# One reset of the running score sum per attention unit, row maxima turned through DRAM, and a staggered last block in a decoder layer

## The chip, the core and the metric

The kernel runs on one NeuronCore of one Trainium2 chip, as one program in one launch. The metric is the device time of that program in microseconds. The core has five engines that run side by side and wait for each other by semaphores: TensorE (PE, matmuls; PEld is its weight load), VectorE (DVE), ScalarE (ACT), GpSimd (POOL) and SyncE (SP, which here issues all DMAs).

## The reference, cut to what matters

The input x has 2 batches of 2048 tokens with 512 features, all in float32. The layer has three residual steps:

```
x = x + attention(layernorm(x)) @ Wo.T     # 16 heads of 32, rotary angles on Q and K
x = x + gelu(layernorm(x) @ ctx.T) @ ctx   # ctx: 77 rows of 512 for each batch
x = x + clip(layernorm(x) @ sign(W).T * scale + bias, -100, 100)
```

Attention is full (2048 by 2048 scores for each head), with a softmax over the keys.

## The kernel before

For each batch the kernel first projects and then attends; what follows attention is cut into small pieces that run in the background of later work.

*Projection* (`project_batch`). The 16 chunks of 128 tokens are taken in turn: layer norm, transposition, K, Q and V matmuls, `rotate` with the `cos` and `sin` tables (lines 207 to 219), and transposition of Q and K into `att.q` and `att.k`, which hold features on partitions, in four blocks of 512 tokens. The last part (lines 254 to 274) has its TensorE and VectorE order written out by hand.

*Attention* (`Attention.run`). A unit is a block of queries, a group `g` of four heads (their 32 features lie on the four strips of 32 partitions) and a half block of 256 queries: 4 x 4 x 2 = 32 units per batch, 64 in all. A unit takes 8 steps (`STEPS`), and a step works on two chunks of 128 keys, which `chunk(i, c)` gives as key block `i % 4`, first half of the block for steps 0 to 3 and second half for steps 4 to 7. A step has two half steps, one for heads 0 and 1, one for heads 2 and 3. In each half, TensorE computes scores into `st`, ScalarE exponentiates them into `pw` (line 705), GpSimd adds the two key chunks into `sm` (line 707), and TensorE multiplies `pw` by the values (`weigh`, line 583) and sums `sm` with ones (`total`, line 597), both for earlier steps.

The scores are kept as a running sum in PSUM. `lower` (line 545) starts a tile of `st` with minus the row maximum, from a tile `mrow` of three bfloat16 parts on partitions. In the first step that follows, `scores` adds the product with the keys of block 0, and in later steps the product with a *difference* of key blocks (`dk`, made in `key_steps`), so that the same PSUM tile turns into the scores of the next keys. `lower` runs in steps 0 and 4.

The row maxima come from a second product, with queries on partitions (`maxima`, line 459): four matmuls of 512 columns per step into `ps` and four VectorE reductions (line 484) into `mx`. They run `AHEAD` = 10 steps ahead of the scores; the first ten of a batch are done in the projection, in the order in which `open_block` puts them into `due` and `lead` takes them out. When a unit's maxima are complete (the end of step 5), `split_maxima` takes the maximum over the key blocks on VectorE and splits it into three bfloat16 parts on GpSimd (lines 493 to 497), and `turn_maxima` brings them onto partitions: by a transposing DMA from SyncE (line 504), and for the first unit of a batch, on TensorE (line 508).

`divide` takes reciprocals and products at a unit's end (lines 607 to 624). In `run` the orders of TensorE, VectorE, ScalarE and GpSimd are written out by hand, as the statements are emitted. Outside, and for SyncE throughout, a planner orders the instructions, by the order of emission and its own estimate of when each is ready.

*After attention* (`after_attention`, line 312). A generator with a `yield` after each piece: output projection and residual (`add_to_x`), layer norm, the 77 context rows with a GELU from products and a tanh (lines 387 to 405), and the sign-weight product with scale, bias, clip and residual (lines 370 to 378). `background` takes pieces from `queue` in the gaps of attention and projection. `side()` gives the engine of the simple operations: GpSimd in general, VectorE in the last `AHEAD` steps of a batch (`free`) and after all attention (`alone`). The four chunks of the last query block of batch 1 go to `tail` instead, one generator each; after attention the last loop of the function runs one piece of each in turn.

*Buffers.* `big` (for `pw`) and `sums` (for `sm`) have three buffers, `ps_t` (for `st`) four and `ps_s` (for `ps`) three.

Of the kernel before, what the change touches and what calls it, by code (L numbers as in the profile page):

```python
# [9 lines left out]
F32 = mybir.dt.float32  # L10
# [6 lines left out]
P = 128  # L17
# [8 lines left out]
HQ = 256  # L26
NU = NB * ND * 2
STEPS = NCH // 2
AHEAD = STEPS + 2
SCALE = 1.0 / math.sqrt(DK)  # L30
EPS = 1e-5
MAX_VAL = 100.0
# [4 lines left out]
def decoder_layer(  # L37
# [48 lines left out]

    x_next = [load_x(0, 0), load_x(0, 1)]
    qkv = load_qkv()
    cos = const.tile([P, NCH, DK // 2], F32, tag="cos", name="cos")
    sin = const.tile([P, NCH, DK // 2], F32, tag="sin", name="sin")  # L90
    nc.sync.dma_start(cos, rope_cos.rearrange("(p c) d -> p c d", p=P))
    nc.sync.dma_start(sin, rope_sin.rearrange("(p c) d -> p c d", p=P))

    ident = const.tile([P, P], F32, tag="ident", name="ident")
    make_identity(nc, ident)
# [7 lines left out]
    nc.scalar.activation(minus_half, ones[:, :CPB], AF.Identity, scale=-0.5)  # L103


    mts = []
    for n in range(2):
        mt = const.tile([P, 2, 4, DK], BF16, tag=f"mt{n}", name=f"mt{n}")
        nc.vector.memset(mt, 0.0)
        mts.append(mt)  # L110

    late = {}

# [63 lines left out]

    def project_batch(b, ahead, att, xnt, wk, wq, wv):  # L180
# [25 lines left out]

        def rotate(ch, a, ps, r):
            half = [P, H, DK // 2]
            cs = cos[:, ch, None, :, None].to_broadcast(half + [2])
            sn = sin[:, ch, None, :].to_broadcast(half)  # L210
# [70 lines left out]

    def side():
        return nc.vector if alone or free else nc.gpsimd


    attending = []
# [25 lines left out]
    def after_attention(b, blk, ot, first, end):  # L312
# [41 lines left out]
        def feed_forward(c, pt):  # L354
            parts = [work_tile([P, D], name, F32R) for name in ("high", "low")]
            parts = [part.rearrange("p (i t) -> p i t", t=P) for part in parts]
            nc.scalar.copy(parts[0], pt)
            nc.vector.tensor_sub(parts[1], pt, parts[0])
            yield True
            pf = bank([P, D], "pf")  # L360
            for k, part in enumerate(parts):
                for i in range(ND):
                    nc.tensor.matmul(  # L363
                        pf,
                        part[:, i, :],
                        wf[:, i, :],
                        start=(k == 0 and i == 0),
                        stop=(k == 1 and i == ND - 1),
                    )
            y = work_tile([P, D], "y")  # L370
            nc.vector.tensor_mul(y, pf, fs)
            yield False
            side().tensor_add(y, y, fb)
            yield False
            side().tensor_scalar(y, y, -MAX_VAL, MAX_VAL, ALU.max, ALU.min)
            side().tensor_add(xs[c], xs[c], y)
            nc.sync.dma_start(tokens(out[b], blk * CPB + first + c), xs[c])
            yield False

# [11 lines left out]
        nc.scalar.copy(h, ph)  # L391
        yield False
        u = work_tile([C, n * P], "u")
        side().tensor_mul(u, h, h)
        yield False
        side().tensor_scalar(u, u, 0.044715, 1.0, ALU.mult, ALU.add)
        side().tensor_mul(u, u, h)
# [4 lines left out]
        side().tensor_scalar(u, u, 1.0, 0.5, ALU.add, ALU.mult)  # L402
        side().tensor_mul(u, u, h)
        yield False
        yield True

# [38 lines left out]
    class Attention:  # L445
# [13 lines left out]
        def maxima(self, n, heads):  # L459
# [25 lines left out]

            return reduce

        def split_maxima(self, u):
            mx = self.mx.pop(u)
            neg = small.tile([P, 2, 4], F32, tag="neg", name="neg")  # L490
            nc.vector.tensor_reduce(neg, mx, AX.X, ALU.max, negate=True)
            mt = mts[u % 2]
            nc.gpsimd.tensor_copy(mt[:, :, :, 0], neg)
            nc.gpsimd.tensor_tensor(neg, neg, mt[:, :, :, 0], ALU.subtract)
            nc.gpsimd.tensor_copy(mt[:, :, :, 1], neg)
            nc.gpsimd.tensor_tensor(neg, neg, mt[:, :, :, 1], ALU.subtract)
            nc.gpsimd.tensor_copy(mt[:, :, :, 2], neg)


        def turn_maxima(self, u):  # L500
            mt = mts[u % 2]
            mrow = small.tile([P, 2, P], BF16, tag="mrow", name="mrow")
            if u > 0:
                nc.sync.dma_start_transpose(mrow, mt.rearrange("p c h d -> p (c h d)"))
            else:
                pt = ps_s.tile([P, 2, P], BF16, tag="s", name="ptm")
                for c in range(2):
                    nc.tensor.transpose(
                        pt[:, c, :], mt[:, c].rearrange("p h d -> p (h d)"), ident_b
                    )  # L510
                nc.vector.tensor_copy(mrow, pt)
            self.mrow[u] = mrow.rearrange("p c q -> p (c q)")

        def key_steps(self):
            self.dk = [None] + [
                const.tile([P, ND, BLK], F32, tag=f"w{n}", name=f"dk{n}") for n in "kqv"
            ]

            def differences(g):
# [12 lines left out]
            for _ in differences(0):  # L534
                pass
            queue.append(others())


        @staticmethod
# [19 lines left out]
        def scores(self, u, i, heads, c):  # L559
            qb, g, hf = self.units[u]  # L560
            kb, kc = divmod(self.chunk(i, c), CPB)
            keys = self.dk[kb] if kb else self.k[kb]
            for h in heads:
                r = self.rows[h]
                nc.tensor.matmul(  # L565
                    self.st[h][:, c, :],
                    keys[r, g, kc * P : (kc + 1) * P],
                    self.q[qb][r, g, hf * HQ : (hf + 1) * HQ],
                    start=False,
                    stop=True,  # L570
                    skip_group_check=True,
                )
# [74 lines left out]
        def run(self):  # L647
# [37 lines left out]
            for t in range(NU * STEPS):  # L685
# [10 lines left out]
                pw = big.tile([P, 4, 2, HQ], F32, tag="s", name="pw")  # L696
                sm = sums.tile([P, 4, HQ], F32, tag="sm", name="sm")
                for heads, others in (((0, 1), (2, 3)), ((2, 3), (0, 1))):
                    if i % NB == 0:
                        self.lower(u, heads)  # L700
                    self.scores(u, i, heads, 0)
                    reduce = self.maxima(t + AHEAD, others)
                    self.scores(u, i, heads, 1)
# [6 lines left out]
                    if heads[0] == 0:  # L710
                        first_half()
                        finish()
                        if u >= NU - ND:
                            background(1)
                        elif t % 2 == 1:
                            background(1, light=True)
                    else:
                        finish()
                        second_half()
                        if prev is not None and prev[1] == STEPS - 1:  # L720
                            finish()
# [15 lines left out]
    xnt = turn(norm(x_next, 0, 0, nc.vector))  # L737
    for b in range(B):
        att = Attention(b)
        project_batch(b, x_next, att, xnt, *qkv)  # L740
        if b == 0:
            late_loads()
        load_ctx(b)
        xnt = att.run()
        if b + 1 < B:
            x_next = att.x_next
            qkv = load_qkv()
    alone.append(True)
# [51 lines left out]
```

## Time and profile before

| | |
|---|---|
| time, median of 3 runs | 2693.01 us (2692.51 to 2693.29) |
| the profiled execution's own time | 2693.15 us |
| its span, first to last instruction | 2691.0 us |
| TensorE busy | 2668.3 us |
| GpSimd, VectorE, ScalarE busy | 1732.8, 1710.0, 1321.0 us |
| projection of batch 0 ends, first L550 | 212.4 us |
| first L550 of batch 1 | 1544.9 us |
| tail, first `po` to the end of the span | 2643.7 to 2691.0 us |
| mean granted TensorE clock | 0.998 |

The profile is of one execution. Times in it are in microseconds from the start of its span. A timeline row gives start, duration, engine, source line, operation, output<-inputs, shapes and count (merged neighbours), and in square brackets the idle time of that engine before it with the instruction that ended the idle time. "L550" is line 550 of the kernel before. A float32 matmul appears as two instructions.

### The profile page before, as it was taken

To read this page: it belongs to the slowest core of one execution; us is meant where nothing else is said; L and a number is where in the kernel's file an instruction comes from. 1 tells how busy PE (TensorE), PEld (TensorE's weight loads), DVE (VectorE), ACT (ScalarE), POOL (GpSimd) and SP (SyncE) were. 2 spreads that over 40 slices of the span, in tenths; PEclk is the share of its full clock that TensorE was granted. 3 is DMA by queue.
4 is the path that set the end of the run, shared out by engine and by line. 5 is a ranking of instruction groups with operands and counts; after the bars stand their busy time and mean duration, and the time that the engine had idled before them with its cause. 6 is when DMAs were issued, how large, how long until landed. Compare 5 with 4: busy or idle time off the path is not lost.

```text
span 2691.0 us, 70222 instructions
## 1 busy us (share of the span) xinstructions
PE 2668.3 (99%) x30756; PEld 1490.3 (55%) x30756; DVE 1710.0 (64%) x2863; ACT 1321.0 (49%) x2394; POOL 1732.8 (64%) x1876
## 2 busy tenths in 40 slices
PE   8999999999999999999999999999999999999998
PEld 4445555555555555555554455555565555555555
DVE  3447777676766766676344477766767667766754
ACT  2115555455546554555422155555555455546553
POOL 3227777567857785677543287766687567857772
PEclk9999999999999999999999999999999999999999
DMA  3010000000000000000201000000000000000000
GB/s 126 24 32 2 5 4 4 4 4 18 20 3 4 12 28 3 4 12 26 73 25 40 5 4 4 4 4 4 4 27 12 4 4 19 19 4 4 19 19 17
DMA packets 38019, 43.54 MB, mean 16 GB/s; under 512 B 20662, under 2 KB 20918, under 8 KB 37712
## 3 DMA queue, kind: packets, MB, share of 16 engines
q1 hardware_dynamic: 37712, 39.05, 4.8%
q8 instruction: 241, 3.95, 0.6%
q14 instruction: 66, 0.54, 0.1%
HBM read 26.58 MB, written 8.39 MB: 13 GB/s over the span
## 4 chain that ended last, share of the span: by engine, by line
PE 98%; DVE 1%; DMA 0%; issue 0%; ACT 0%; POOL 0%; SPq 0%; POOLq 0%; ACTq 0%
PE st L565 23%; PE acc L583 22%; PE ps L472 18%; PE acc L597 8%; PE po L382 4%; PE pk L183 4%; PE pq L183 4%; PE pv L183 4%; PE st L550 3%; PE pf L363 2%; PE pt L345 1%; PE po L408 1%; PE ptqk L191 1%; PE ph L389 1%; PE pt L173 1%; DMA wk<-in_wk_t_dram 0%
## 5 line engine op out<-in xcount | busy, mean ns | idle before, releaser
L707 POOL TENSOR_TENSOR sm<-pw 128x512 f32<-128x512 f32 x1024 | 1295.2, 1272 | 599.5 <-ACT pw L705 596.8
L484 DVE TENSOR_REDUCE mx<-ps 128x1 f32<-128x512 f32 x2048 | 1308.9, 682 | 513.0 <-PE ps L472 509.1
L705 ACT ACTIVATE pw<-st 128x512 f32<-128x512 f32 x2048 | 1111.4, 595 | 947.0 <-PE ps L472 619.4
L472 PE MATMUL ps<-k,q 32*128 32x512 f32 x4096 | 1187.8, 640 | 0.0
L583 PE MATMUL acc<-pw,v 128*32 128x256 f32 x8192 | 655.1, 391 | 0.0
L597 PE MATMUL acc<-sm,ones 128*32 128x128 f32 x7680 | 388.8, 280 | 0.0
L583 PEld LDWEIGHTS acc<-pw,v 128*32 128x32 f32 x8192 | 162.5, 108 | 396.6 <-issue 378.3
L472 PEld LDWEIGHTS ps<-k,q 32*128 32x128 f32 x4096 | 352.4, 183 | 20.2 <-issue 13.8
L597 PEld LDWEIGHTS acc<-sm,ones 128*32 128x32 f32 x7680 | 248.6, 110 | 153.2
L565 PE MATMUL st<-q,dkk 32*128 32x256 f32 x2048 | 291.2, 400 | 0.0
L565 PE MATMUL st<-q,dkq 32*128 32x256 f32 x2048 | 290.0, 400 | 0.0
L565 PE MATMUL st<-q,dkv 32*128 32x256 f32 x2048 | 290.0, 400 | 0.0
L565 PE MATMUL st<-q,k 32*128 32x256 f32 x2048 | 262.8, 375 | 0.0
L565 PEld LDWEIGHTS st<-q,dkk 32*128 32x128 f32 x2048 | 175.8, 184 | 89.5 <-issue 51.3
L565 PEld LDWEIGHTS st<-q,dkq 32*128 32x128 f32 x2048 | 173.0, 184 | 79.9 <-issue 54.1
L565 PEld LDWEIGHTS st<-q,dkv 32*128 32x128 f32 x2048 | 175.0, 184 | 58.6 <-issue 26.3
L565 PEld LDWEIGHTS st<-q,k 32*128 32x128 f32 x2048 | 195.4, 187 | 14.0
L219 POOL TENSOR_TENSOR r<-r 128x512 f32<-128x512 f32 x64 | 81.1, 1268 | 161.8 <-DVE r L218 151.5
L617 DVE RECIPROCAL num<-num 128x128 f32<-128x128 f32 x128 | 120.4, 942 | 53.5 <-ACT num L611 53.5
L137 DVE BATCH_NORM_STATS2 st<-x 128x6 f32<-128x512 f32 x96 | 65.4, 686 | 91.7 <-DMA x<-in_x_dram 91.4
L183 PE MATMUL pk<-wk,xnt 128*128 128x512 f32 x256 | 118.2, 606 | 2.4 <-ACT xnt L175 1.3
L382 PE MATMUL po<-wo,q 128*128 128x512 f32 x256 | 117.4, 603 | 0.0
(109 smaller groups left out, 1784.9 us busy)
## 6 DMA issues: line engine op xcount, KB each, us to landing
x<-in_x_dram SPq DMA_DIRECT2D x64, 256.0 KB, 2.8
out_dram<-x SPq DMA_DIRECT2D x32, 256.0 KB, 2.0
wk<-in_wk_t_dram SPq DMA_DIRECT2D x2, 1024.0 KB, 7.8
wq<-in_wq_t_dram SPq DMA_DIRECT2D x2, 1024.0 KB, 9.9
wv<-in_wv_t_dram SPq DMA_DIRECT2D x2, 1024.0 KB, 5.5
wo<-in_wo_t_dram SPq DMA_DIRECT2D x1, 1024.0 KB, 9.9
wf<-in_wf_t_dram SPq DMA_DIRECT2D x1, 1024.0 KB, 5.0
mrow<-mt SPq DMA_TRANSPOSE x62, 2.3
```

What stands on the lines that cost most here:

```text
L183: nc.tensor.matmul(dst, xnt[:, i, :], w[:, i, :], start=(i == 0), stop=(i == ND - 1))
L219: nc.gpsimd.tensor_add(r[:, 0, a], r[:, 0, a], r[:, 1, a])
L382: nc.tensor.matmul(ps, ot[:, i, cols], wo[:, i, :], start=(i == 0), stop=(i == ND - 1))
L472: nc.tensor.matmul(ps, self.q[qb][self.rows[h], g, q0 : q0 + P], self.k[kb][self.rows[h], g, :], start=True, stop=True,)
L484: nc.vector.tensor_reduce(mx[:, qc, h, kb : kb + 1], ps, AX.X, ALU.max)
L550: nc.tensor.matmul(self.st[h], ones_b[r, :], mrow[r, None, :].to_broadcast([DK, 2, HQ]), start=True, stop=False, skip_group_check=True,)
L565: nc.tensor.matmul(self.st[h][:, c, :], keys[r, g, kc * P : (kc + 1) * P], self.q[qb][r, g, hf * HQ : (hf + 1) * HQ], start=False, stop=Tr ...
L583: nc.tensor.matmul(acc[self.rows[h], 0, :], self.v[self.chunk(i, c)][:, d0 : d0 + DK], pw[:, h, c, :], start=(i == 0 and c == 0), stop=(i ...
L597: nc.tensor.matmul(acc[self.rows[h], 1, part], ones, sm[:, h, part], start=False, stop=(i == STEPS - 1), skip_group_check=True,)
L617: nc.vector.reciprocal(num[:, 1, part], num[:, 1, part])
L705: nc.scalar.activation(pw[:, h], self.st[h], AF.Exp, scale=SCALE)
L707: nc.gpsimd.tensor_add(sm[:, hs, :], pw[:, hs, 0, :], pw[:, hs, 1, :])
```

## The change

It has four parts.

1. `lower` runs in step 0 alone. In step 4 the sum goes on with a wrap difference, the second half of key block 0 minus the first half of key block 3, made on GpSimd once for each head group as its units come up (`wrap_around`).
2. `AHEAD` grows from 10 to 11. `split_maxima` does its first two operations after `neg`, and `turn_maxima` the rest, on VectorE; the turn is called a half step later, in the first half of step 5. It transposes 32 by 32 blocks on VectorE, writes them to DRAM and reads them back with eight DMAs, each of three rows for one head and one half of the queries. The first unit of a batch still goes over TensorE. `mrow` is now a pair of constant tiles.
3. The tables `cos` and `sin` become one tile in the pool `sums`, loaded once for each batch, after the weights.
4. In the tail, a new chunk starts every four turns of the last loop (`STAGGER`). The products of the GELU, and the bias and residual of all but the last chunk, run on GpSimd there (`aside`, `closing`).

```diff
-AHEAD = STEPS + 2
+STAGGER = 4
+AHEAD = STEPS + 3
...
+    def load_angles():
+        angles = sums.tile([P, 2, NCH, DK // 2], F32, tag="sm", name="angles")
+        for n, table in enumerate((rope_cos, rope_sin)):
+            nc.sync.dma_start(angles[:, n], table.rearrange("(p c) d -> p c d", p=P))
+        return angles
...
+    first_mt = zeros([P, 2, 4, DK], "first_mt")
+    mts = [zeros([P, 4, DK // 4], f"mt{n}") for n in range(2)]
+    mrows = [zeros([P, 2, P], f"mrow{n}") for n in range(2)]
+    dram = ctx.enter_context(tc.tile_pool(name="dram", bufs=2, space=bass.MemoryType.DRAM))
...
+    def aside():
+        return nc.vector if free else nc.gpsimd
...
+            closing = side() if first + c == CPB - 1 else aside()
             nc.vector.tensor_mul(y, pf, fs)
             yield False
-            side().tensor_add(y, y, fb)
+            closing.tensor_add(y, y, fb)
             yield False
             side().tensor_scalar(y, y, -MAX_VAL, MAX_VAL, ALU.max, ALU.min)
-            side().tensor_add(xs[c], xs[c], y)
+            closing.tensor_add(xs[c], xs[c], y)
...
-        side().tensor_mul(u, h, h)
+        aside().tensor_mul(u, h, h)
...
         def split_maxima(self, u):
             mx = self.mx.pop(u)
             neg = small.tile([P, 2, 4], F32, tag="neg", name="neg")
             nc.vector.tensor_reduce(neg, mx, AX.X, ALU.max, negate=True)
-            mt = mts[u % 2]
-            nc.gpsimd.tensor_copy(mt[:, :, :, 0], neg)
-            nc.gpsimd.tensor_tensor(neg, neg, mt[:, :, :, 0], ALU.subtract)
-            nc.gpsimd.tensor_copy(mt[:, :, :, 1], neg)
-            nc.gpsimd.tensor_tensor(neg, neg, mt[:, :, :, 1], ALU.subtract)
-            nc.gpsimd.tensor_copy(mt[:, :, :, 2], neg)
+            if u == 0:
+                parts = [first_mt[:, :, :, n] for n in range(3)]
+            else:
+                by_head = mts[u % 2][:, :, 0:6].rearrange("p h (c n) -> p c h n", n=3)
+                parts = [by_head[:, :, :, n] for n in range(3)]
+            nc.vector.tensor_copy(parts[0], neg)
+            nc.vector.tensor_tensor(neg, neg, parts[0], ALU.subtract)
+            self.rest = neg, parts
 
         def turn_maxima(self, u):
+            neg, parts = self.rest
+            nc.vector.tensor_copy(parts[1], neg)
+            nc.vector.tensor_tensor(parts[2], neg, parts[1], ALU.subtract)
+            mrow = mrows[u % 2]
...
-                nc.sync.dma_start_transpose(mrow, mt.rearrange("p c h d -> p (c h d)"))
+                square = small.tile([P, DK], BF16, tag="square", name="square")
+                nc.vector.transpose(square, mts[u % 2].rearrange("p h n -> p (h n)"))
+                rows = dram.tile([P, DK], BF16, tag="rows", name="rows")
+                nc.sync.dma_start(rows, square)
+                by_row = rows.rearrange("(a h n) i -> n a h i", a=4, h=4)
+                for h in range(4):
+                    for c in range(2):
+                        nc.sync.dma_start(
+                            mrow[h * DK : h * DK + 3, c].rearrange("n (a i) -> n a i", a=4),
+                            by_row[3 * c : 3 * c + 3, :, h, :],
+                        )
...
+        def wrap_around(self, g):
+            if self.wrap is None or self.wrap[0] != g:
+                d = small.tile([P, BLK // 2], F32, tag="wrap", name="wrap")
+                nc.gpsimd.tensor_sub(
+                    d, self.k[0][:, g, BLK // 2 :], self.k[NB - 1][:, g, : BLK // 2]
+                )
+                self.wrap = g, d
...
-            keys = self.dk[kb] if kb else self.k[kb]
+            if i == NB:
+                keys = self.wrap[1][:, None, :].to_broadcast([P, ND, BLK // 2])
+                kc = c
+            else:
+                keys = self.dk[kb] if kb else self.k[kb]
...
-                    if i % NB == 0:
+                    if i == 0:
                         self.lower(u, heads)
+                        self.wrap_around(self.units[u][1])
...
+                        if (t + AHEAD) % STEPS == 0 and u + 1 < NU:
+                            self.turn_maxima(u + 1)
...
                         if (t + AHEAD) % STEPS == STEPS - 1 and u + 1 < NU:
                             self.split_maxima(u + 1)
-                            self.turn_maxima(u + 1)
...
-    queue += tail
-    while queue:
+
+    turns = 0
+    while queue or tail:
+        if tail and turns % STAGGER == 0:
+            queue.append(tail.pop(0))
+        turns += 1
         for piece in list(queue):
```

More of the change, by code (lines that the diff above doesn't have):

```diff
@@ L88, in decoder_layer @@
     qkv = load_qkv()
[L89 to L92, printed above, removed]
+    def load_angles():
[3 more added lines that the diff above has]
+        return angles
+    angles = load_angles()
     ident = const.tile([P, P], F32, tag="ident", name="ident")
@@ L103, in decoder_layer, with zeros @@
     nc.scalar.activation(minus_half, ones[:, :CPB], AF.Identity, scale=-0.5)
[L106 to L110, printed above, removed]
+    def zeros(shape, name):
+        t = const.tile(shape, BF16, tag=name, name=name)
+        nc.vector.memset(t, 0.0)
+        return t
+    first_mt = zeros([P, 2, 4, DK], "first_mt")
+    mts = [zeros([P, 4, DK // 4], f"mt{n}") for n in range(2)]
+    mrows = [zeros([P, 2, P], f"mrow{n}") for n in range(2)]
+    dram = ctx.enter_context(tc.tile_pool(name="dram", bufs=2, space=bass.MemoryType.DRAM))
     late = {}
@@ L176, in turn, with project_batch @@
         return xnt
-    def project_batch(b, ahead, att, xnt, wk, wq, wv):
+    def project_batch(b, ahead, att, xnt, angles, wk, wq, wv):
         def times(dst, xnt, w, part=range(ND)):
@@ L208, in rotate @@
             half = [P, H, DK // 2]
-            cs = cos[:, ch, None, :, None].to_broadcast(half + [2])
-            sn = sin[:, ch, None, :].to_broadcast(half)
+            cs = angles[:, 0, ch, None, :, None].to_broadcast(half + [2])
+            sn = angles[:, 1, ch, None, :].to_broadcast(half)
             pairs = ps.rearrange("p (h i t) -> p h i t", i=DK // 2, t=2)
@@ L393, in after_attention @@
         u = work_tile([C, n * P], "u")
-        side().tensor_mul(u, h, h)
+        aside().tensor_mul(u, h, h)
         yield False
-        side().tensor_scalar(u, u, 0.044715, 1.0, ALU.mult, ALU.add)
-        side().tensor_mul(u, u, h)
+        aside().tensor_scalar(u, u, 0.044715, 1.0, ALU.mult, ALU.add)
+        aside().tensor_mul(u, u, h)
         yield False
@@ L401, in after_attention @@
         yield False
-        side().tensor_scalar(u, u, 1.0, 0.5, ALU.add, ALU.mult)
-        side().tensor_mul(u, u, h)
+        aside().tensor_scalar(u, u, 1.0, 0.5, ALU.add, ALU.mult)
+        aside().tensor_mul(u, u, h)
         yield False
@@ L491, in split_maxima @@
             nc.vector.tensor_reduce(neg, mx, AX.X, ALU.max, negate=True)
-            mt = mts[u % 2]
-            nc.gpsimd.tensor_copy(mt[:, :, :, 0], neg)
-            nc.gpsimd.tensor_tensor(neg, neg, mt[:, :, :, 0], ALU.subtract)
-            nc.gpsimd.tensor_copy(mt[:, :, :, 1], neg)
-            nc.gpsimd.tensor_tensor(neg, neg, mt[:, :, :, 1], ALU.subtract)
-            nc.gpsimd.tensor_copy(mt[:, :, :, 2], neg)
-        def turn_maxima(self, u):
[L501 to L505, printed above, removed]
+            if u == 0:
[6 more added lines that the diff above has]
+            self.rest = neg, parts
+        def turn_maxima(self, u):
+            neg, parts = self.rest
+            nc.vector.tensor_copy(parts[1], neg)
+            nc.vector.tensor_tensor(parts[2], neg, parts[1], ALU.subtract)
+            mrow = mrows[u % 2]
+            if u == 0:
                 pt = ps_s.tile([P, 2, P], BF16, tag="s", name="ptm")
@@ L508, in turn_maxima @@
                     nc.tensor.transpose(
-                        pt[:, c, :], mt[:, c].rearrange("p h d -> p (h d)"), ident_b
+                        pt[:, c, :], first_mt[:, c].rearrange("p h d -> p (h d)"), ident_b
                     )
                 nc.vector.tensor_copy(mrow, pt)
+            else:
[10 more added lines that the diff above has]
+                        )
             self.mrow[u] = mrow.rearrange("p c q -> p (c q)")
@@ L519, in key_steps @@
             ]
+            self.wrap = None
             def differences(g):
@@ L561, in scores @@
             kb, kc = divmod(self.chunk(i, c), CPB)
-            keys = self.dk[kb] if kb else self.k[kb]
+            if i == NB:
+                keys = self.wrap[1][:, None, :].to_broadcast([P, ND, BLK // 2])
+                kc = c
+            else:
+                keys = self.dk[kb] if kb else self.k[kb]
             for h in heads:
@@ L739, in decoder_layer @@
         att = Attention(b)
-        project_batch(b, x_next, att, xnt, *qkv)
+        project_batch(b, x_next, att, xnt, angles, *qkv)
         if b == 0:
@@ L747, in decoder_layer @@
             qkv = load_qkv()
+            angles = load_angles()
     alone.append(True)
-    queue += tail
-    while queue:
+    turns = 0
[3 more added lines that the diff above has]
+        turns += 1
         for piece in list(queue):
```

## The prediction

> **What bounds the kernel now.** I read the page first (busy shares, then the chain that ended last), then the timeline of TensorE and VectorE inside one attention unit, then the timeline of the last 47 us, last the SyncE rows.
>
> ```profile
> PE 2668.3 (99%) x30756; PEld 1490.3 (55%) x30756; DVE 1710.0 (64%) x2863; ACT 1321.0 (49%) x2394; POOL 1732.8 (64%) x1876
> ...
> PE 98%; DVE 1%; DMA 0%; issue 0%; ACT 0%; POOL 0%; SPq 0%; POOLq 0%; ACTq 0%
> ```
>
> TensorE is the bound nearly everywhere; 2691.0 - 2668.3 = 22.7 us of its idle time is all that any other engine can give back directly. POOL at 64% is on no chain. The TensorE timeline:
>
> ```profile
> 804.33 0.39 PE L550 MATMUL st<-mrow,ones_b 32*128 32x512 bf16 x2
> ...
> 806.30 0.39 PE L550 MATMUL st<-mrow,ones_b 32*128 32x512 bf16 x2
> ...
> 808.27 0.48 PE L565 MATMUL st<-q,dkk 32*128 32x256 f32 x2
> ...
> 810.12 0.49 PE L565 MATMUL st<-q,dkk 32*128 32x256 f32 x2
> ```
>
> A half step that begins with L550 lasts 806.30 - 804.33 = 1.97 us, twice; the first half without it 810.12 - 808.27 = 1.85, and over the trace second halves without it last 1.90. VectorE in another unit:
>
> ```profile
> 264.67 1.29 DVE L484 TENSOR_REDUCE mx<-ps 128x1 f32<-128x512 f32 x2 [0.57 <-PE ps L472]
> 266.07 0.19 DVE L491 TENSOR_REDUCE neg<-mx 128x8 f32<-128x32 f32 x1
> 266.57 1.29 DVE L484 TENSOR_REDUCE mx<-ps 128x1 f32<-128x512 f32 x2 [0.31 <-PE ps L472]
> ...
> 279.66 0.94 DVE L617 RECIPROCAL num<-num 128x128 f32<-128x128 f32 x1
> 280.52 1.22 DVE L484 TENSOR_REDUCE mx<-ps 128x1 f32<-128x512 f32 x2
> ```
>
> VectorE is idle 0.57 us in a half step, 0.31 in the one that holds `neg`. More than that makes the reductions late, and with three buffers behind `ps` TensorE soon waits: after the two reciprocals of a unit a half of 1.86 lasts 2.22. So VectorE has no slack beyond that gap. The tail:
>
> ```profile
> 2643.66 14.00 PE L382 MATMUL po<-wo,q 128*128 128x512 f32 x32
> ...
> 2667.22 1.10 PE L408 MATMUL po<-ctx,sparev 77*128 77x512 f32 x2 [0.49 <-DVE sparev L403]
> 2672.42 1.12 PE L345 MATMUL pt<-ident,sparek 128*128 128x128 f32 x4 [4.10 <-ACT sparek L339]
> ```
> ```profile
> 2672.00:2676.00 4.00, 3.42 (x15) 3.03 (x16) 1.15 (x7) 3.54 (x7) 0.96 (x2) 0.50 0.01 2
> ```
>
> The four chunks go in step, so TensorE waits for all of them at once (4.10 us); the second view, of four microseconds by engine, shows a granted clock of 0.50 just after (its third number from the end). The last residual ends at 2688.03. The queue that the rows will use:
>
> ```profile
> L504 SPq DMA_TRANSPOSE mrow<-mt x62: 1168/1173/1892, 237.4 to 2606.9; - x62
> ...
> DMA to landing us min/median/max: 2.3/2.3/4.2
> ```
>
> **The change, part by part.** The sum is against the profiled execution: span 2691.0, its own time 2693.15, 2.15 us around it; the median of the three runs, 2693.01, is 0.14 lower.
>
> *Unit-long differences.* Of the two pairs of half steps with L550 in each of 64 units one pair loses it: (1.97 + 1.97) - (1.86 + 1.90) = 0.18 us, x64 = -11.5. The wrap difference is 20 subtractions per batch on POOL, 40 in all; between L707's 1.27 us for 512 columns and L620's 0.46 for 128, about 0.73 each, needed four steps (15 us) later. POOL has 0.6 us free per half step and also loses five small operations per unit (0.20 to 0.22 us each): 0 on the path. Without that cover the cost would be 40 x 0.73 = 29.
>
> *One step more ahead.* AHEAD 11 puts maxima step 10 into the projection, before steps 3 and 7, for 8 more `ps` instructions (1.07 us) and 4 reductions (2.47 us). Today the order there is step 3 (reduced 1536.15 to 1538.6), step 7, the last `pv` at 1539.93, L550 at 1544.88. With a third group ahead of that `pv`, step 7's matmuls wait for step 3's reductions at 1542.5; `pv` starts there, 2.6 us later, in the first batch 3.0, since the sign conversions share VectorE. In attention the removed step gives nothing back: a half lasts 1.85 without maxima and 1.86 with. +5.5.
>
> *Split and turn on VectorE.* After `neg` follow two small operations in the gap of step 4 and two and a transpose in that of step 5. L146 and L148 on VectorE take 0.15 and 0.16, 0.03 apart. First gap: 0.31 left, 0.37 wanted. For a 128x32 transpose no row is near; the zeroing of 128x32 took 0.09, the skill's page "VectorE: DVE Perf Modes", section "The three transpose paths", gives 311 ns for 128x128 bf16, and I take 0.2, since the copy of 128x256 took 0.29. Second gap: 0.57 left, 0.6 wanted. 0.05 us per unit, x64 = +3; the ends are 0 and 0.35 (what 0.3 us too much cost after the reciprocals), +22. Background's `bn_stats` (0.87 with its aggregate) meets these as it met `neg`. For unit 0 the VectorE chain is 0.8 us shorter than POOL's 1.6, behind the late `pv`: 0.
>
> *Rows through DRAM.* SyncE gets nine issues instead of one; plain loads there occupy it 0.33 us each, the transpose 1.17. Backward from L550: `neg` came 6.9 us before it (234.90 to 241.8), the turn comes half a step earlier, at 8.8, the square is done at about 8.2. Write: 2.0 to land (as `out` does); four reads for the first two heads: 3 x 0.33 more, and 2.3; with hops 5.5. Slack 2.7 us; the other four reads land 1.3 later and are needed 2.0 later. Queued behind them on SyncE are x loads and out stores, none due within 3 us. Cost 0; if uncovered, 62 us per us of lateness. Here a rule speaks against the change. The row: landing 2.3, at worst 4.2. The Trainium skill, "DMA: Bandwidth & Descriptors", section "Rules for kernel authors", wants the hardware transpose and calls a rearranged plain DMA 19 times slower: 19 x 2.3 = 44 us, 36 over the slack, x62 = +2200. Each run here stays 64 bytes contiguous, since VectorE transposes the blocks first, so I take the row; no run shows the strided case.
>
> *Angles.* They now share `sums` and are loaded again for batch 1, behind the third weight (issued at 1325.81, 5.5 us to land). The first rotation was at 1332.72; it may be 1 to 2 us late, and `pk` keeps its buffer, of which the fourth successor comes at 1343. SyncE issues two more (0.7 us) ahead of an x load. With the extra semaphores before L550: +0.5, ends 0 and 5.
>
> *The tail.* Emitted four pieces apart, the chunks' `po` stay first in line except where pieces of earlier chunks are ready: two transposes (0.5 each) and two `ph` (1.0 each) enter, so the last `po` ends at 2657.66 + 3.0 = 2660.7. From there one chunk's chain by today's rows: to its normalised x 3.7 (2657.69 to 2661.43), transpose and copy 1.3, `ph` and copy 1.5, products on POOL 0.40 + 2 x 0.46 + 2 x 0.29 (from the 77x512 and 77x256 rows, 1.27 and 0.73) with tanh and hops 2.7, `po` 1.1, statistics and x 3.6, transpose 0.8, parts 1.4, `pf` 2.3, last four on VectorE 2.5: 20.9, so 2681.6, and 1.4 for POOL's 1.27 us bias and residual of earlier chunks in its way: 2683.0 against 2688.03. The row with clock 0.50 bears on this: the skill's page "TensorE: Matmul & The Clock Gate", section "Part 1: The HAM clock gate", halves the clock after an idle window of about 3.4 us. By the rule alone, with no gap that long, the sixteen transposes return from 3.7 us to 2.0 and the tail gains 1.7; by my walk, which counts them at full speed, 5.0. I take -5.5, ends -9 and +1 (POOL's clumsier operations in series).
>
> Sum: -11.5 + 5.5 + 3 + 0.5 - 5.5 = -8.0. 2693.15 - 8.0 = 2685.15; with the 0.14, 2685.0.
>
> **The rivals.** (1) *The removed L550 is eaten*: the extra step 5.5, VectorE 5, angles 1, no gain in the tail: -11.5 + 11.5 = 0, 2693. For it: three small costs, all on engines without slack. Against: the 4.10 us gap. (2) *VectorE becomes the bound of steps 4 to 6*, on the slower side: at 0.35 us per unit the sum is -8 + 19 = +11, 2704. It decides from 0.17 us per unit (-8 + 8). For: the reciprocals' stalls. Against: the gaps nearly fit. (3) *The rows land late*: both landings at 4.2 give 9.4 us for 8.2, +1.2 x 62 = 74, 2759. For: such landings occurred; against: seldom, beside large loads. (4) *The change doesn't do what it says*: if the halves freed of L550 fall only to VectorE's 1.90, 0.14 x 64 = 9, 2687.5.
>
> **How the numbers follow.** The forecast 0.55 (own range 2680 to 2691), rival 4 0.10, rival 1 0.20, rival 2 0.11, rival 3 0.04. About 0.2%, 5.4 us, is what a measurement of this kernel can tell from no change: faster is below 2687.6, slower above 2698.4. Faster: most of the forecast and half of rival 4, 0.57; same 0.27; slower 0.16. The range 2676 to 2697 takes in -9 in the tail and VectorE up to 0.2 us per unit, and leaves out rival 3 and the worst of rival 2.
>
> **What would show it.** L550's bf16 matmuls x256; halves of step 4 at 1.86 and 1.90; the unit of 31.09 us (237.43 to 268.52) near 30.95. L550 from `mrow` of batch 1 at about 1547.5 after that batch's earlier start. No wait of L550 on `mrow`'s DMAs above 0.5 us. The tail from the last attention matmul to the last residual 39 us, not 44, with no clock of 0.50. Wrong: waits of `ps` on `mx` after steps 4 and 5, or L550 waiting for landings in most units.

## The result: 70 us slower

The changed kernel takes 2762.91 us (median of four runs, 2762.36 to 2763.99), the kernel before 2692.8, measured beside it: ratio 1.0261, interval 1.0243 to 1.0278. The prediction was 2685, with a range up to 2697.

The span is 2759.9 us. The busy shares of the page after, and its chain of work that ended last:

```profile
PE 2724.5 (99%) x30500; PEld 1469.8 (53%) x30500; DVE 1835.8 (67%) x3158; ACT 1322.3 (48%) x2394; POOL 1717.2 (62%) x1622
...
PE 95%; DVE 3%; issue 0%; POOL 0%; ACT 0%; DMA 0%; ACTq 0%
```

TensorE has 256 instructions fewer, as meant, and yet its busy time is 56 us longer. That is no new work: the ends of matmuls are modelled, and waits between them can be counted as busy (of the half step from 266.10 to 268.78 below, which lost 0.8 us, all 2.68 us count as busy). So the busy share does not tell where the time went. On the chain VectorE went from 1% to 3%. The summed waits of one instruction for another (waiting <- awaited: us, times, longest), before and then after, show the buffer in question:

```profile
PEld ps L472 <- DVE mx L484: 1.8, 3, 0.8
```
```profile
PEld ps L490 <- DVE mx L502: 53.4, 69, 1.6
```

These are the same two lines of code. The weight loads of `maxima` wait for VectorE to have read a `ps` buffer, 69 times instead of 3. What keeps VectorE? Its groups after, by line and shape (count | busy us, mean ns of one | idle before):

```profile
L516 DVE CAST mt<-neg 128x8 bf16<-128x8 f32 x62 | 63.3, 1021 | 2.2
...
L523 DVE TENSOR_TENSOR mt<-neg,mt 128x8 bf16<-128x8 f32 x62 | 28.3, 456 | 2.1
L522 DVE CAST mt<-neg 128x8 bf16<-128x8 f32 x62 | 24.3, 392 | 0.0
...
L517 DVE TENSOR_TENSOR neg<-neg,mt 128x8 f32<-128x8 f32 x62 | 17.7, 286 | 2.1
...
L534 DVE STREAM_TRANSPOSE square<-mt 128x32 bf16<-128x32 bf16 x62 | 13.1, 211 | 2.3 <-DVE mt L523 0.2
L510 DVE TENSOR_REDUCE neg<-mx 128x8 f32<-128x32 f32 x64 | 11.9, 186 | 2.2
...
L516 DVE CAST first_mt<-neg 128x8 bf16<-128x8 f32 x2 | 0.4, 186 | 0.1
```

The first and the last row are one line of code on eight elements per partition: 1021 ns in 62 units, 186 in the first unit of each batch, which is split in the projection. The reduction `neg` just before it reads four times as many elements in 186. The timeline of one unit, cut to the rows that matter, shows what the copy lasts until:

```profile
264.24 0.48 PE L611 MATMUL st<-q,dkk 32*128 32x256 f32 x2
...
264.76 1.27 POOL L754 TENSOR_TENSOR sm<-pw 128x512 f32<-128x512 f32 x1 [0.46 <-ACT pw L752]
264.84 0.19 DVE L510 TENSOR_REDUCE neg<-mx 128x8 f32<-128x32 f32 x1
265.06 1.02 DVE L516 CAST mt<-neg 128x8 bf16<-128x8 f32 x1
266.10 0.48 PE L611 MATMUL st<-q,dkk 32*128 32x256 f32 x2
266.11 0.17 DVE L517 TENSOR_TENSOR neg<-neg,mt 128x8 f32<-128x8 f32 x1
266.20 1.28 DVE L502 TENSOR_REDUCE mx<-ps 128x1 f32<-128x512 f32 x2
266.78 1.26 POOL L754 TENSOR_TENSOR sm<-pw 128x512 f32<-128x512 f32 x1 [0.74 <-ACT pw L752]
267.40 0.69 DVE L522 CAST mt<-neg 128x8 bf16<-128x8 f32 x1
268.12 0.20 DVE L523 TENSOR_TENSOR mt<-neg,mt 128x8 bf16<-128x8 f32 x1
268.35 0.21 DVE L534 STREAM_TRANSPOSE square<-mt 128x32 bf16<-128x32 bf16 x1
268.59 0.34 SPq L536 DMA_DIRECT2D rows<-square  x1
268.78 0.48 PE L611 MATMUL st<-q,dkq 32*128 32x256 f32 x2
```

GpSimd's running sum lasts from 264.76 to 266.03; the copy L516 starts in the middle of it and ends at 266.08. The next sum ends at 268.04, the copy L522 at 268.09. The two do not share data. Over the whole trace, L516 began 62 times while GpSimd ran an instruction, and 62 times it ended 37 to 47 ns after that instruction; the two executions with GpSimd idle took 184 and 188 ns. The other copy and the two subtractions do the same when they meet GpSimd: L522 in 33 of 64 cases (582 ns on average, against 175 in the others), L523 in 15 (1273 against 195), L517 in 7 (1181 against 172). The transpose (211 ns) and the reduction (186 ns) take the same time beside GpSimd as alone.

The half steps pay for it: the half from 264.24 lasts 1.86 us, the one from 266.10, in which the reductions are a microsecond late, 2.68. Averaged over halves that hold no background piece, the second half of step 5 went from 1.90 to 2.40 us and the first of step 6 from 1.86 to 2.25. That is 0.89 us, times 62 units 55 us of the 70. Over all halves, those with background pieces too, the two grew by 0.72 and 0.36 us on average, 69 us in 64 units, of which step 4, freed of its reset, gave back 10.

The page of before already held the sign of it. VectorE's clip and residual by form (count | busy us, mean ns | idle before):

```profile
L376 DVE TENSOR_TENSOR x<-x,spareq 128x512 f32<-128x512 f32 x4 | 2.7, 686 | 0.0
L376 DVE TENSOR_TENSOR x<-x,y 128x512 f32<-128x512 f32 x2 | 2.4, 1214 | 0.0
L375 DVE TENSOR_SCALAR y<-y 128x512 f32<-128x512 f32 x2 | 2.2, 1094 | 0.0
L375 DVE TENSOR_SCALAR spareq<-spareq 128x512 f32<-128x512 f32 x4 | 1.7, 422 | 0.0
```

The same operation at the same size takes 1.1 us in the attention steps, where GpSimd works, and 0.42 in the tail, where it does not. Where one group has two durations, the shorter belongs to a condition.

### The profile page after: what moved, and what is told of

The parts are those of the page before. It is cut to its first block, busy times and chain, and to the rows that moved or that the text cites. A ratio compares the mean times of both kernels' runs of the same rounds, so it can differ in the third digit from the quotient of the medians.

```text
span 2759.9 us, 70900 instructions
## 1 busy us (share of the span) xinstructions
PE 2724.5 (99%) x30500; PEld 1469.8 (53%) x30500; DVE 1835.8 (67%) x3158; ACT 1322.3 (48%) x2394; POOL 1717.2 (62%) x1622
## 4 chain that ended last, share of the span: by engine, by line
PE 95%; DVE 3%; issue 0%; POOL 0%; ACT 0%; DMA 0%; ACTq 0%
PE st L611 22%; PE acc L629 21%; PE ps L490 19%; PE acc L643 8%; PE pk L196 4%; PE pq L196 4%; PE pv L196 4%; PE po L400 4%; PE pf L380 2%; PE st L592 1%; DVE mx L502 1%; PE pt L362 1%; PE po L426 1%; PE ph L407 1%; PE ptqk L204 1%; DVE mt L516 1%
## 5 line engine op out<-in xcount | busy, mean ns | idle before, releaser
L754 POOL TENSOR_TENSOR sm<-pw 128x512 f32<-128x512 f32 x1024 | 1298.7, 1273 | 706.7 <-ACT pw L752 703.1
L490 PE MATMUL ps<-k,q 32*128 32x512 f32 x4096 | 1251.8, 639 | 8.3 <-DVE mx L502 8.1
L490 PEld LDWEIGHTS ps<-k,q 32*128 32x128 f32 x4096 | 375.4, 183 | 72.7 <-DVE mx L502 53.4
L611 PE MATMUL st<-q,dkk 32*128 32x256 f32 x2048 | 302.6, 404 | 0.0
L611 PE MATMUL st<-q,wrap 32*128 32x256 f32 x1024 | 144.9, 400 | 0.0
L611 PE MATMUL st<-q,k 32*128 32x256 f32 x1024 | 131.6, 374 | 0.0
```

What stands on the lines that cost most here:

```text
L490: nc.tensor.matmul(ps, self.q[qb][self.rows[h], g, q0 : q0 + P], self.k[kb][self.rows[h], g, :], start=True, stop=True,)
L611: nc.tensor.matmul(self.st[h][:, c, :], keys[r, g, kc * P : (kc + 1) * P], self.q[qb][r, g, hf * HQ : (hf + 1) * HQ], start=False, stop=Tr ...
L754: nc.gpsimd.tensor_add(sm[:, hs, :], pw[:, hs, 0, :], pw[:, hs, 1, :])
```

## Experiments

Each kernel's ratio is against the kernel before, measured beside it.

**Theory: a VectorE copy or subtraction waits until GpSimd's instruction has ended. Rival: VectorE simply has too much work in steps 4 to 6.** The first test puts the split back on GpSimd, at the places where the change has it.

```diff
-            nc.vector.tensor_copy(parts[0], neg)
-            nc.vector.tensor_tensor(neg, neg, parts[0], ALU.subtract)
+            engine = nc.vector if u == 0 else nc.gpsimd
+            engine.tensor_copy(parts[0], neg)
+            engine.tensor_tensor(neg, neg, parts[0], ALU.subtract)
```

(and the same for the two operations in `turn_maxima`)

> The changed kernel with the four small operations of the split (two copies to bfloat16, two subtractions) on GpSimd at the same two places in the order; the block transpose stays on VectorE. Theory (a VectorE copy waits until the GpSimd operation that is running has ended): the 1.02 us copies and all waits of TensorE on the reductions at steps 5 and 6 go, 70 us: 2763 - 70 = 2693, between 2688 and 2698. Rival (the step more ahead, the turn in step 5 or the way through DRAM is what costs, and VectorE's copies are only where it shows): above 2745.

2763.89 us, ratio 1.0264 (1.025 to 1.0278): nothing gained. The waits in this form are gone and another has come, in its summed waits and its timeline:

```profile
DVE square L536 <- POOL mt L525: 116.8, 62, 3.4
```
```profile
267.26 1.27 POOL L756 TENSOR_TENSOR sm<-pw 128x512 f32<-128x512 f32 x1 [0.24 <-ACT pw L754]
268.48 0.22 POOL L524 CAST mt<-neg 128x8 bf16<-128x8 f32 x1
268.78 0.23 POOL L525 TENSOR_TENSOR mt<-neg,mt 128x8 bf16<-128x8 f32 x1
269.04 0.21 DVE L536 STREAM_TRANSPOSE square<-mt 128x32 bf16<-128x32 bf16 x1 [1.80 <-POOL mt L525]
269.88 0.69 PE L490 MATMUL ps<-k,q 32*128 32x512 f32 x1 [0.21 <-DVE mx L502]
```

GpSimd does L524 and L525 only after the sum that stands ahead of them, VectorE's transpose waits 1.80 us for them with the reductions behind it, and TensorE runs out of `ps`. The experiment exchanged one wait for another, so it decided nothing. The repair gives GpSimd all four operations in `split_maxima`, half a step earlier, and leaves `turn_maxima` the transpose:

> The changed kernel with all four small operations of the split on GpSimd straight after neg in step 4, so that they are done (2.3 us after neg in the profile of before) when VectorE comes to the block transpose in step 5. The run with the split in two places on GpSimd took 2763.9, and its VectorE waits 1.80 us at the transpose for GpSimd's last subtraction: one wait took the place of the other. Theory (any wait of VectorE beyond its gap of 0.57 us, for GpSimd's port or for GpSimd's result, stops TensorE): with neither wait 2763 - 66 = 2697, between 2690 and 2702, near the 2698.6 of the four reductions. Rival (moving the split to GpSimd leaves the cost, because something else in steps 5 and 6 costs it): above 2740.

2701.46 us, ratio 1.0031 (1.002 to 1.0042). The second half of step 5 is back at 1.89 us, the first of step 6 at 1.96. With the work off VectorE 61 us are back, which both theories allow. So the next kernel leaves the amount of VectorE's work as it was and exchanges the kind: four reductions, which do not wait in the trace, in place of two copies and two subtractions. Parts two and three of each maximum are left out. The first unit of each batch keeps its copies and subtractions.

```diff
-            nc.vector.tensor_copy(parts[0], neg)
-            nc.vector.tensor_tensor(neg, neg, parts[0], ALU.subtract)
+                nc.vector.tensor_reduce(parts[0], mx, AX.X, ALU.max, negate=True)
+                nc.vector.tensor_reduce(neg, mx, AX.X, ALU.max, negate=True)
...
-            nc.vector.tensor_copy(parts[1], neg)
-            nc.vector.tensor_tensor(parts[2], neg, parts[1], ALU.subtract)
+                for _ in range(2):
+                    nc.vector.tensor_reduce(neg, mx, AX.X, ALU.max, negate=True)
```

> The changed kernel with the four small VectorE operations of the split replaced by four reductions of the same 128x8 output (0.19 us each in the profile, 0.19 also while GpSimd runs); the first writes the bfloat16 part, the others nothing that is used, so the second and third part of each maximum are left out. Theory (it is the kind of operation that waits for GpSimd): VectorE has as many instructions as before but none of them waits; 0.78 + 0.59 us in two gaps of 0.57, some 0.2 to 0.3 us per unit: 2700 to 2712. Rival (VectorE has simply too many instructions in those two gaps): near 2760.

2698.61 us, ratio 1.002 (1.0013 to 1.0027), a little under the range expected. The same number of VectorE instructions, each of 0.18 us, costs 64.3 us less. The rival is out. Last, one single instruction of this kernel is turned back into the copy:

```diff
-                nc.vector.tensor_reduce(parts[0], mx, AX.X, ALU.max, negate=True)
+                nc.vector.tensor_copy(parts[0], neg)
```

> The kernel with four reductions (2698.6), but its first reduction after neg is again the copy of neg to bfloat16, as in the changed kernel; the second and third part of each maximum stay left out. One instruction of the same shape in the same place differs. Theory (the copy waits for the end of GpSimd's running sum, 0.84 us more than its own 0.19 on average in the changed kernel, and what passes the gap of 0.57 us stops TensorE): 0.3 to 0.8 us per unit, 2698.6 + 20 to 50 = 2719 to 2749. Rival (the copies after it, or all four together, cost): 2699 to 2704.

2733.96 us, ratio 1.0154 (1.014 to 1.0168): 35 us for an instruction of 128x8. The group of line 520 in the kernel with four reductions, then in this one:

```profile
L520 DVE TENSOR_REDUCE mt<-mx 128x8 bf16<-128x32 f32 x62 | 11.4, 184 | 0.0
```
```profile
L520 DVE CAST mt<-neg 128x8 bf16<-128x8 f32 x62 | 63.2, 1019 | 2.2
```

and in the same order the wait of TensorE's loads for VectorE:

```profile
PEld ps L490 <- DVE mx L502: 10.5, 22, 1.6
```
```profile
PEld ps L490 <- DVE mx L502: 38.4, 48, 1.6
```

The copy lasts 0.835 us longer, times 62 is 52 us, and 35 of them reach the end. On average over all units the second half of step 5 alone grew by 0.55 us, 35 us in 64; the remainder is, by my reading, taken up in VectorE's gap.

**The other way about.** The kernel before, with nothing but its five split operations taken from GpSimd to VectorE (`nc.gpsimd` to `nc.vector` in lines 493 to 497):

> The kernel before with its five small operations of the split on VectorE in their old place, nothing else changed. Theory (the first copy waits for GpSimd's running sum): about 1.0 us of waiting and 0.9 us of work for a gap that has 0.31 left, so 0.8 to 1.5 us per unit: 2693 + 50 to 95 = 2743 to 2788. Rival (the cost of the changed kernel needs its other parts): 2693 to 2705.

2841.66 us, ratio 1.0549 (1.0535 to 1.0563): +149, far more than expected. Its timeline shows why (L707 and L523 are GpSimd's sums and key differences):

```profile
272.25 1.03 DVE L493 CAST mt<-neg 128x8 bf16<-128x8 f32 x1
273.19 1.26 POOL L523 TENSOR_TENSOR dkv<-k,k 128x512 f32<-128x512 f32 x1
273.31 1.17 DVE L494 TENSOR_TENSOR neg<-neg,mt 128x8 f32<-128x8 f32 x1
274.42 1.26 POOL L707 TENSOR_TENSOR sm<-pw 128x512 f32<-128x512 f32 x1
274.52 1.20 DVE L495 CAST mt<-neg 128x8 bf16<-128x8 f32 x1
276.77 1.22 PE L472 MATMUL ps<-k,q 32*128 32x512 f32 x1 [2.35 <-DVE mx L484]
```

Operations in a row each meet a new GpSimd instruction: L494 begins 0.12 us after L523 and ends just after it, L495 begins 0.10 after L707 and ends just after it. TensorE then stands idle for 2.35 us, and the mean granted clock of the run is 0.979, against 0.998 before; it was 0.50 from 276.60 to 283.20, from the end of this stall on. By an estimate from the two means, (0.998 - 0.979) x 2840.7 = 54 us of full clock are missing, so up to about a third of the +149 may be the clock's and not the wait's own.

**The parts that were meant to gain.** The unit-long differences by themselves, in the kernel before (`if i % NB == 0` to `if i == 0`, the wrap difference, and the angles in the sums' pool, whose room it needs):

> The kernel before with the unit-long differences alone (L550 once per unit and the wrap difference on GpSimd), and the angle tables in the shared pool, without which it has no room. Step 4's halves of the changed kernel (1.865 and 1.895 us against 1.971 and 1.968) say -0.18 us per unit: 2693 - 11.5 + 0.5 = 2682. Rival (the wrap difference on GpSimd costs something, or the angles come late): 2686 to 2693.

2683.11 us, ratio 0.9963 (0.9949 to 0.9976): -9.5. The staggered start of the last four chunks alone:

```diff
-    queue += tail
-    while queue:
+    while queue or tail:
+        if tail and turns % 4 == 0:
+            queue.append(tail.pop(0))
+        turns += 1
```

> The kernel before with the last four chunks four pieces apart, everything of theirs on VectorE as before. In the changed kernel the tail takes 53.0 us for 47.3. Theory (GpSimd's bias and residual stand in the way of the last chunk's norm, on GpSimd itself and, through VectorE's clip that waits for them, on VectorE): the offset alone gains, 2686 to 2690. Rival (the offset itself is what costs, since the chunks' pieces interleave badly): 2695 to 2699.

2695.12 us, ratio 1.0009 (1.0001 to 1.0017): +2.5, where I expected a gain. And the products, bias and residual on GpSimd alone (`aside` and `closing`), with the chunks in step:

> The kernel before with the tail's products, bias and residual on GpSimd, the four chunks in step as before. The offset alone took 2695.1 and both 2696.4. Theory (what hurts is VectorE's written order, in which operations that wait for GpSimd or for an earlier chunk stand before the last chunk's): without the offset every chunk waits for the slower products, 0.25 us more each of three and again for bias and residual, 2695 to 2699. Rival (GpSimd relieves VectorE, on which the four chunks queue for 9 us at the end): 2688 to 2691.

2700.0 us, ratio 1.0026 (1.0016 to 1.0036): +7.4. Both together:

> The kernel before with the offset of the last four chunks and with products, bias and residual on GpSimd, nothing else. The tail of the changed kernel is 5.7 us longer, and the offset alone gave +2.5. Theory (GpSimd's slower operations in series, and VectorE's clip waiting for them in order, add to the offset's cost): 2697 to 2700. Rival (GpSimd's share is neutral): 2695.

2696.42 us, ratio 1.0015 (1.0008 to 1.0021): +3.7, between the two ranges. The larger step ahead alone (`AHEAD = STEPS + 3`; its split stays on GpSimd and its turn on the transposing DMA):

> The kernel before with AHEAD = STEPS + 3 and nothing else. In the changed kernel the first L550 came 1.9 us later in batch 0 and, counted from the last chunk's keys, 2.6 us later in batch 1. Theory (a third group of reductions ahead of the last values, nothing back in attention): +4.5, 2697. Rival (the later end of the maxima work gives it back): 2692 to 2694.

2701.16 us, ratio 1.0032 (1.002 to 1.0044): +8.5, more than expected.

**A better version.** The prediction had noticed that the two reciprocals at a unit's end, 0.94 us each, make the reductions late. The kernel before with four reciprocals of half the width:

```diff
-            for c in range(2):
-                part = slice(c * P, (c + 1) * P)
+            w = HQ // 4
+            for c in range(4):
+                part = slice(c * w, (c + 1) * w)
```

> The kernel before with the two reciprocals of 128 columns at a unit's end (0.94 us each) cut into four of 64 columns, one in each of the half steps from 1 to 2, and the products on GpSimd likewise. Theory (VectorE beyond its gap of about 0.57 us per half step is paid by TensorE in the same or the next half): 0.5 us each nearly fit, and the 0.25, 0.36 and 0.10 us that the halves lose there go for the most part: 0.4 to 0.65 us per unit, 2693 - 25 to 42 = 2651 to 2668. Rival (only waits for GpSimd stop TensorE, plain VectorE work doesn't): 2693, or above for the extra instructions.

2676.48 us, ratio 0.9941 (0.9928 to 0.9953): -15.7. The gain is only a part of what I expected. The reciprocals now last 0.54 us each and the first half of step 2 fell from 2.14 to 1.86 us, as meant, but its second half fell only from 1.96 to 1.89 and the second half of step 3 rose from 1.91 to 1.98. With the unit-long differences, and nothing else of the change:

> The unit-long differences alone (2683.1) with the reciprocals in quarters. Theory: both gains add, as they lie in different steps: 2642 to 2660. Rival (as above): 2683.

2667.07 us, ratio 0.9907 (0.9892 to 0.9922): -25.1, faster than both kernels. The range missed as the one before it had, but the two gains add up (9.5 + 15.7 = 25.2); it is the best version here.

## Why the prediction was wrong

**The step that failed** is "L146 and L148 on VectorE take 0.15 and 0.16, 0.03 apart. First gap: 0.31 left, 0.37 wanted." Those rows stem from the tail, where GpSimd is nearly idle. In the gap GpSimd runs sums of 1.27 us, and the first copy took 1.02 us. I wrote +3 with an end of +22 (0.05 us per unit, though the excesses of the two gaps, 0.06 and 0.03, make 0.09, +6). With four reductions in the same places 2698.6 - 2695.3 = +3.3 is left (2695.3 is 2692.6 and the three other parts, -9.5 + 8.5 + 3.7), so a few us for the work itself are not contradicted; the intervals of the four kernels leave this remainder open by some 5 us. The missing term is the wait: 2762.9 - 2698.6 = 64.3 us, 1.04 per unit.

Rival 2 had the place (VectorE becomes the bound of steps 4 to 6, `ps` waiting on `mx`) and not the price: its 0.35 us per unit was taken from the reciprocals, which are long by themselves, while here short operations became long because of when they ran. Rival 1, the gain eaten by small costs, describes the kernel without the wait better than the forecast does: with four reductions it ended at +6.0.

The trace of before could have given that price. The line L148, from which I took 0.16 us, stands there with two durations:

```profile
L148 DVE TENSOR_TENSOR stats<-stats 128x1 f32<-128x1 f32 x9 | 1.4, 160 | 4.2 <-POOL stats L147 4.2
L148 DVE TENSOR_TENSOR stats<-stats 128x2 f32<-128x2 f32 x1 | 1.2, 1237 | 4.2 <-POOL stats L147 4.2
```

The one of 1237 ns is the only one on VectorE in attention. It began at 1289.85, 0.06 us after one of GpSimd's sums had begun, and ended 0.02 us after that sum's end. And in the unit whose `neg` the prediction showed, from 266.07 to 266.26, GpSimd's timeline has

```profile
265.92 1.27 POOL L707 TENSOR_TENSOR sm<-pw 128x512 f32<-128x512 f32 x1 [0.47 <-ACT pw L705]
```

The Trainium skill, "SBUF — State Buffer", section "Who interferes with whom", has the rule: GpSimd and VectorE share one pair of SBUF ports, which whichever instruction issues first holds until it is finished; VectorE's copy, cast and `tensor_scalar` can take that pair, an instruction with two inputs in SBUF contends as well with a GpSimd instruction that reads SBUF, and on this chip a `tensor_reduce` never does. By that, a copy behind `neg` is held to 267.19, 0.93 us, where a gap of 0.31 was left: about 0.6 us per unit, +40, from the first copy alone, an estimate (one copy cost 35). The traces agree for the copies (1021 ns against 186), the subtractions (1181 against 172), `tensor_scalar` (1094 against 422) and the reductions (186 either way). That ports are the reason is the page's statement; the traces show who waits for whom and how long. I had weighed another rule against the change, the one on rearranged transfers (+2200 us, an estimate from the figure of its page), and that one did not bear.

**Unit-long differences: right.** `lower`'s matmuls fell from 512 to 256. Step 4's halves went from 1.97 and 1.97 to 1.87 and 1.90, 0.18 us per unit. By itself -9.5, against -11.5 + 0.5 for it and the angles. GpSimd's wrap difference takes 737 ns, 0.73 estimated, and costs nothing visible. Rival 4 falls.

**AHEAD: right for the projection, 3 us too small in all.** Forecast +5.5, measured +8.5. In the kernel with this part alone the projection of batch 0 lost 2.4 us (forecast 3.0) and that of batch 1 2.6 (forecast 2.6). In attention, which I had put at nothing, the two batches became 1.0 and 1.3 us longer. That accounts for the profiled execution, 2700.05 us and so 6.9 above that of before; the 1.6 us up to the median's +8.5 are in no trace.

**Rows through DRAM: right.** SyncE and TensorE after, in the unit shown above:

```profile
268.59 0.34 SPq L536 DMA_DIRECT2D rows<-square  x1
270.08 2.94 SPq L540 DMA_DIRECT2D mrow<-rows  x8
```
```profile
276.65 0.39 PE L592 MATMUL st<-mrow,ones_b 32*128 32x512 bf16 x2
```

The square is ready at 268.56, 8.1 us before `lower` starts (forecast 8.2). The eight reads are issued in 2.94 us, and no wait of `lower` for a DMA is in the trace. Rival 3 falls. That this holds does not say that the plain path would beat the transposing DMA: no run compares the two alone.

**The tail: wrong in sign.** Forecast -5.5, measured +3.7. The -5.5 was more than either of my workings gave, 5.0 and 1.7. The first step was right: with the stagger alone the last `po` of the projection ended at 2661.99, where I had 2660.7. From there I walked one chunk's chain by itself, 20.9 us and 1.4 for others in its way. It took 2690.84 - 2661.99 = 28.85. The four chunks share VectorE, 7.2 and 8.4 us busy in the two 10 us windows from 2664, and it does their pieces in the written order, so the last chunk's statistics stand behind other chunks' bias and clip. I had put the queue at 1.4 us for GpSimd and at nothing for VectorE. In the changed kernel both queues do it, as VectorE's, GpSimd's and TensorE's rows show:

```profile
2743.86 1.29 POOL L391 TENSOR_TENSOR sparek<-sparek,fb 128x512 f32<-128x512 f32 x1 [0.63 <-DVE stats L151]
2745.19 0.43 DVE L393 TENSOR_SCALAR sparek<-sparek 128x512 f32<-128x512 f32 x1 [0.74 <-POOL sparek L391]
2745.53 0.15 DVE L159 TENSOR_SCALAR stats<-stats 128x1 f32<-128x1 f32 x1
2745.70 1.26 POOL L394 TENSOR_TENSOR x<-x,sparek 128x512 f32<-128x512 f32 x1 [0.55 <-DVE stats L159]
2746.92 0.55 POOL L160 TENSOR_TENSOR stats<-stats,minus_half 128x1 f32<-128x1 f32 x1
2747.50 0.16 DVE L161 TENSOR_TENSOR stats<-stats 128x1 f32<-128x1 f32 x1 [1.82 <-POOL stats L160]
2748.81 1.12 PE L362 MATMUL pt<-ident,spareq 128*128 128x128 f32 x4 [3.03 <-ACT spareq L356]
```

L159 belongs to the last chunk, whose aggregate ended at 2743.87. It stands behind L393, which waits for GpSimd's bias of another chunk: 1.66 us. GpSimd's L160 then stands behind that chunk's residual, 1.2 us more. TensorE idles 3.03 us, and in the five microseconds from 2749 its granted clock is 0.50 again, which I had named as a sign of being wrong. I had taken a gap of about 3.4 us to be needed for that; here 3.03 us were enough, and 2.35 in the kernel with five operations on VectorE. From the first `po` to the end of the span the tail takes 53.0 us, 47.3 before.

**The sum.** -9.5 + 8.5 + 3.7 + 3.3 + 64.3 = +70.3. The first three terms come from a kernel each and the last from the exchange of four operations; +3.3 is the remainder, so that the sum closes by construction. It holds the rows through DRAM too, which no run has alone, and whatever the parts do to each other.

## What to carry to other kernels

A small VectorE copy, or an operation with two inputs in SBUF, waited here for what was left of GpSimd's instruction, so it is not priced by a row from a stage in which GpSimd is idle: look first whether the same line has two durations. A reduction in its place did not wait. A chain of one chunk walked alone is a lower bound: count on every engine what the other chunks have written ahead of it.

## What the hardware showed beside that

- The waiting operations of the changed kernel end 25 to 55 ns after GpSimd's instruction in 116 of 117 cases, so almost none of their 0.17 to 0.2 us is left when they are let go.
- Whether the wait falls on one operation or on five decides the price: one copy cost 35 us, two copies and two subtractions 64, five operations (three copies, two subtractions) in the kernel before 149, the last with stalls of TensorE such as the 2.35 us above and a granted clock of 0.979.
- A two-input operation with one input in PSUM did not wait: the residual L344 (`x<-po,x`) took 676 ns on average in the 28 cases that began while GpSimd ran an instruction, and 690 in the 31 that met none.
- The wait goes the other way too, as two cases in the trace of before show: GpSimd's product L620 lasted 0.90 us from 1303.30, beside VectorE's residual L376, against 0.46 on average, and L147 lasted 0.99 from 1313.62 beside the next L376, against 0.57.
- `lower` after the change shows 244 short entries in the weight-load queue, 51 ns each, presumably for the semaphores of the eight DMAs. No idle time is put down to them.
